# Routing of the last chunks inside the last pair's passes, the block table ahead of the last bound, x1 loaded during the blocks, 16 result tiles in the gather stage

## The chip, the cores and the metric

The kernel runs on one core of a Trainium2 chip. The metric is the device time of one execution in microseconds (us). Work is spread over the engines of the core: TensorE (PE in the profile; PEld is its loading of weights), VectorE (DVE), ScalarE (ACT), GpSimd (POOL) and SyncE (SP), which here only issues DMAs. DMAs are issued from SP's queue (SPq), ACT's (ACTq) and POOL's. Each engine takes its instructions in order; semaphores tie the engines together.

## The reference, cut to what matters

One transformer block on `x` of 4 sequences x 1024 tokens x 256 channels, modulated by a condition vector:

```
h = layernorm(x) * (1 + ca) + sa
x = x + ga * attn(h)            # gated delta rule, 16 heads of 64
h = layernorm(x) * (1 + cb) + sb
x = x + gb * ffn(h)             # mixture of 8 experts, the best 2 per token

# attn: q, k, v = silu(causal conv of 4 taps (h W)); k normalised; per step
S = clip(a_t * S + b_t * (v_t - a_t * S k_t) k_t^T, -5, 5);   o_t = S q_t
out = (o * silu(h Wg + bg)) Wo

# ffn: the two largest of 8 router logits, softmax over these two
y_e = gelu(h w1_e + b1_e) w2_e + b2_e;    out = p_1 y_e1 + p_2 y_e2
```

The kernel leaves the clip out and proves along the way that it never acts: a bound on every entry of S is carried through the sequence, and the flag `ok` says at the end whether the bound stayed under the limit. Only if it did not, a slow second program (`steps`, `experts`) runs after everything else.

## The kernel before, in words

**Chunks and pairs.** The tokens are cut into 32 chunks; a chunk is 32 tokens of each of the 4 sequences, that is 128 rows on the 128 partitions. Two chunks make a pair, and there are 16 pairs. The loop over the pairs in `chunks` runs several streams side by side: the preparation of the next pair (projections, decays, triangles), the passes through the state of this pair (`z`, `u`, `o`, S, `yT`, `ps_w`, and at the end of a chunk the sum `x<-x,add` at L1036), and the bounds (`ps_ut`, `sides`, the scans at L1096, `worst` at L1104). A stream is a Python generator; a string `PLAN` of one letter per step says which stream issues its next step. So the order of the instructions on PE, DVE, ACT and POOL within this part is written out by hand, and an instruction that waits holds whatever stands behind it on its engine. For the last pair there is nothing to prepare, and only passes, bounds and the streams `l` and `x` remain in the plan. After it come the last chunk's outputs, its `finish` and its bounds.

**Routing.** A finished chunk gets its second layernorm (`statistics`, `normed`, `modulated`), its router logits (`ps_h2`, `ps_l`), the two best experts, its places in the experts' lists (`ps_rk`, a count of the rows before it; `next` carries the counts on from chunk to chunk) and two indirect DMAs that write its 128 rows into `rows_scratch`, one for each expert (L394). The pair loop does this for the chunks finished in the pair before, within the preparation of the next pair. As the last pair prepares nothing, five chunks, 27 to 31, are left over, and they are routed after the last bounds, two at a time, since `ln2_h` has two buffers.

**The flag.** `ext`, `nul` and `ok` (L1202 to L1207) add up `worst` and look for values of S that are not finite; `ps_ok` and `n_safe` turn the flag into a number that the engines load at the very end.

**Blocks.** `blocks` makes a table (L1567 to L1633): how many blocks of 256 rows each expert has, and for each of 39 blocks its expert and its first row. SP loads the two numbers of each block from the table and with them issues the loads of the rows (`hb`, L1649), the weights (`w`, L1651 and L1653) and biases (`b`, L1655 and L1657), three buffers of each. PE transposes the rows (`ps_t`, L1663), multiplies by `w1` (`ps_hm`, L1670), ACT applies Gelu (L1677), PE multiplies by `w2` (`ps_yb`, L1682), DVE adds the bias (L1686), and POOL's queue writes the result to `outs_scratch` (L1687). Rows, logits' differences and the gate lie on other partitions than the last stage wants them, so small DMAs on ACT's queue copy them, eight for each of `at_out`, `dif_out` and `gate_out` (L1641).

**Gathers.** For each of the 32 chunks, two indirect DMAs on POOL fetch the two results of its 128 tokens (`y`, L1699), ACT and DVE weight and add them (L1705 to L1710) to `x1o`, which SP loads from `x_out_scratch` (L1695), and ACT's queue stores the sum (L1711). Each of these tiles has four buffers. The weights `prob` come from a sigmoid on ACT (L1692), whose function table is another than Gelu's.

The instructions of `blocks` are put in order by a scheduler, those of `chunks` not. A DMA that SP or ACT issues signals on one of eight semaphores, which the program goes round; an issue waits until the DMA before it on the same semaphore has landed. POOL's indirect DMAs have eight such semaphores of their own.

## Time and profile before

| | us |
|---|---|
| runs before the change, median (lowest to highest) | 2398.57 (2388.15 to 2409.16) |
| the profiled execution's own time | 2395.64 |
| its span | 2393.9 |
| last sum of chunk 31 (L1036) ends | 1906.5 |
| last bounds end (L1104) | 1926.6 |
| chunks 27 to 31 routed on DVE | 1924.9 to 1972.9 |
| first load of the first block | 1984.30 |
| last write of a block's result is issued | 2291.08 |
| first and last gather | 2296.02, 2382.79 |

All times within the profile are counted from the start of the span. The page of the profile gives busy time by engine and the costliest groups of instructions; the timeline gives the single rows, each with its start, its duration, and in brackets the idle time of its engine just before it and what ended that. Over the whole span PE is busy for 76% and DVE for 67%, but the shares differ by stage: until about 1900 several engines share the work, from 1995 to 2291 PE is nearly always busy, and after 2291 it stands still. The clock that TensorE was granted is 0.834 of full speed in the mean.

### The profile page before, as it was taken

The numbers are of one execution on the slowest core, as the hardware profiler recorded it, in microseconds if no ns is written. First come the engines' busy times: TensorE is split into PE (matmuls) and PEld (weight loads), VectorE is DVE, ScalarE is ACT, GpSimd is POOL, SyncE is SP. The second block draws the span as 40 slices with busy tenths as digits, with TensorE's granted clock in tenths as the row PEclk, the third lists the DMA queues.
The fourth block names the chain that finished last, engine by engine and source line by source line (L and its number), as shares of the span: only waits on it lengthen the run. The fifth ranks groups of instructions, "written<-read, shape, count | busy, mean of one in ns | idle before, by whom it ended". The sixth has DMA issues, their size and how long they took to land.

```text
span 2393.9 us, 96754 instructions
## 1 busy us (share of the span) xinstructions
PE 1816.4 (76%) x42550; PEld 1471.7 (61%) x42550; DVE 1598.0 (67%) x3170; ACT 1008.6 (42%) x2005; POOL 1079.2 (45%) x1189
## 2 busy tenths in 40 slices
PE   5777878787878787878787878878786627999920
PEld 3566666566657675666666666766675516888820
DVE  4768687878887878788787878887876332111133
ACT  3343545464545545454545453645453212222211
POOL 1115354647464645456454546464736630000055
PEclk7778889898989898989787888989797758999965
DMA  5523342435353434345343424232323106666645
GB/s 153 155 53 92 92 123 78 140 88 148 92 140 95 134 91 133 98 140 134 92 131 93 120 70 105 85 101 71 97 76 80 42 19 228 226 223 225 216 124 163
DMA packets 321248, 285.37 MB, mean 119 GB/s; under 512 B 112243, under 2 KB 279283, under 8 KB 320435
## 3 DMA queue, kind: packets, MB, share of 16 engines
q1 hardware_dynamic: 304946, 245.08, 36.0%
q0 software_dynamic: 9264, 27.01, 3.3%
q8 instruction: 337, 5.52, 0.9%
q10 hardware_dynamic: 6608, 7.00, 0.9%
q14 instruction: 93, 0.75, 0.1%
HBM read 215.09 MB, written 67.90 MB: 118 GB/s over the span
## 4 chain that ended last, share of the span: by engine, by line
PE 54%; issue 13%; DVE 9%; POOL 8%; ACT 7%; DMA 6%; SPq 2%; another core or an unknown queue 0%; ACTq 0%; POOLq 0%; DVEq 0%
PE ps_q L431 16%; PE ps_hm L1670 6%; PE ps_yb L1682 5%; PE ps_w L1025 3%; PE ps_gt L579 3%; PE ps_kk L647 3%; DMA sc<-g_scratch 3%; PE ps_t L810 3%; PE ps_u L923 2%; PE ps_s L955 2%; DVE kq L443 2%; POOL kq L792 2%; POOL aS L993 2%; PE ps_o L974 2%; PE ps_t L822 1%
## 5 line engine op out<-in xcount | busy, mean ns | idle before, releaser
L443 DVE SCALAR_TENSOR_TENSOR kq<-ps_q,w_conv,kq 128x256 f32<-128x256 f32 x768 | 362.6, 482 | 133.2 <-ACT kq L441 113.2
L431 PE MATMUL ps_q<-hT,w_kq 128*128 128x280 f32 x1024 | 364.7, 506 | 31.5 <-issue 12.0
L431 PEld LDWEIGHTS ps_q<-hT,w_kq 128*128 128x128 f32 x1024 | 232.7, 241 | 109.1 <-issue 21.2
L443 DVE SCALAR_TENSOR_TENSOR v<-ps_q,w_conv,v 128x256 f32<-128x256 f32 x384 | 185.1, 482 | 69.6 <-ACT v L441 59.2
L441 ACT ACTIVATE kq<-ps_q,w_conv 128x256 f32<-128x256 f32 x256 | 143.5, 563 | 200.4 <-PE ps_q L431 198.6
L792 POOL TENSOR_TENSOR kq<-kq,sc 128x512 f32<-128x512 f32 x128 | 177.1, 1404 | 87.4 <-DMA sc<-g_scratch 63.8
L1096 DVE TENSOR_TENSOR_SCAN sides<-aR,sides 128x512 f32<-128x512 f32 x128 | 189.8, 1482 | 37.0 <-POOL sides L1089 36.1
L1088 POOL TENSOR_TENSOR sides<-sides,least 128x512 f32<-128x512 f32 x128 | 193.7, 1513 | 10.0
L431 PE MATMUL ps_q<-hT,w_v 128*128 128x280 f32 x512 | 166.3, 451 | 41.1 <-ACT least L1073 22.6
L1686 DVE TENSOR_TENSOR yb<-ps_yb,b 128x256 f32<-128x256 f32 x78 | 33.1, 425 | 243.8 <-PE ps_yb L1682 243.8
L993 POOL TENSOR_TENSOR aS<-S,last 128x1024 f32<-128x1024 f32 x64 | 128.5, 2008 | 132.5 <-DVE S L962 128.4
L1085 POOL TENSOR_TENSOR sides<-sides,kR 128x512 f32<-128x512 f32 x128 | 166.4, 1300 | 17.4 <-ACT sides L1071 17.3
L1677 ACT ACTIVATE hm<-ps_hm,b 128x256 f32<-128x256 f32 x156 | 73.8, 473 | 221.0 <-PE ps_hm L1670 217.1
L1687 POOL DMA_DIRECT2D outs_scratch<-yb x39 | 27.9, 716 | 285.8 <-DVE yb L1686 276.1
L1670 PE MATMUL ps_hm<-hT,w 128*128 128x256 f32 x624 | 145.1, 386 | 8.5 <-DVE hT L1665 8.5
L579 PE MATMUL ps_gt<-hT,w_gt 128*128 128x256 f32 x512 | 147.4, 411 | 4.4 <-issue 3.1
L1682 PE MATMUL ps_yb<-w,hm 128*128 128x256 f32 x624 | 141.0, 379 | 0.0
L431 PEld LDWEIGHTS ps_q<-hT,w_v 128*128 128x128 f32 x512 | 96.8, 207 | 70.7 <-ACT least L1073 34.5
L810 PE MATMUL ps_t<-Tn,kd 32*32 32x16 f32 x4096 | 63.9, 210 | 96.2 <-issue 56.1
L1670 PEld LDWEIGHTS ps_hm<-hT,w 128*128 128x128 f32 x624 | 118.2, 192 | 29.2 <-DVE hT L1665 13.6
L394 POOL DMA_INDIRECT rows_scratch<-ln_h,at x64 | 64.9, 1015 | 153.3 <-DVE at L391 77.4
L441 ACT ACTIVATE v<-ps_q,w_conv 128x256 f32<-128x256 f32 x128 | 71.9, 562 | 146.6 <-PE ps_q L431 139.2
(211 smaller groups left out, 3953.1 us busy)
## 6 DMA issues: line engine op xcount, KB each, us to landing
w<-in_w SPq DMA_DIRECT2D x78, 512.0 KB
rows_scratch<-zero_row SPq DMA_DIRECT2D x34, 1024.0 KB
w_kq<-in_w_qkv SPq DMA_DIRECT2D x260, 128.0 KB
sc<-g_scratch SPq DMA_DIRECT2D x128, 256.0 KB
w_v<-in_w_qkv SPq DMA_DIRECT2D x129, 128.0 KB
w_gt<-in_w_g SPq DMA_DIRECT2D x258, 64.0 KB
aR<-g_scratch SPq DMA_DIRECT2D x128, 128.0 KB
kR<-g_scratch SPq DMA_DIRECT2D x128, 128.0 KB
```

The source lines that it names most:

```text
L431: nc.tensor.matmul(ps.rearrange("p y t -> p (y t)"), lhsT=w[:, dc], rhs=h_t[:, dc].rearrange("p x b t -> p (x b t)"), start=(dc == 0), sto ...
L441: nc.scalar.activation(o, tap(0), AF.Identity, scale=taps[:, 0:1], bias=taps[:, KC : KC + 1])
L443: nc.vector.scalar_tensor_tensor(o, tap(j), taps[:, j : j + 1], o, op0=ALU.mult, op1=ALU.add)
L579: nc.tensor.matmul(ps, lhsT=wg[:, dc], rhs=self.h_t[:, dc, :, :, KC - 1 :].rearrange("p x b t -> p (x b) t"), start=(dc == 0), stop=(dc == 1),
L792: nc.gpsimd.tensor_tensor(o, o, sc[:, h4 : h4 + 4], ALU.mult)
L810: nc.tensor.matmul(ps[q, n], lhsT=kd[q, n], rhs=Tn[q, n], start=True, stop=True)
L993: nc.gpsimd.tensor_tensor(aS.rearrange("q b h i -> q (b h) i"), S[:, bs].rearrange("q b h i -> q (b h) i"), self.pair.last[self.par][:, bs ...
L1085: nc.gpsimd.tensor_tensor(grow, grow, kR.rearrange("q h b t -> q h (b t)"), ALU.mult)
L1088: nc.gpsimd.tensor_tensor(grow, grow, least, (ALU.subtract, ALU.add)[y])
L1096: nc.vector.tensor_tensor_scan(f, aR.rearrange("q h b t -> q (h b t)"), f, 0.0, ALU.mult, ALU.add)
L1670: nc.tensor.matmul(ps, lhsT=w1[:, dc, fc * P : (fc + 1) * P], rhs=hT[:, dc], start=(dc == 0), stop=(dc == 1),)
L1682: nc.tensor.matmul(ps, lhsT=hm[:, fc, s * P : (s + 1) * P], rhs=w2[:, fc], start=(fc == 0), stop=(fc == 3),)
```

## The change

Four things are changed.

1. *Routing.* A new generator `sent` routes finished chunks one step at a time. In the last pair every second step of the plan is followed by one step of `sent`: first the two chunks that were finished before this pair (27 and 28, together), then 29 and 30, as they get finished. What is left of it runs after the last `finish`, and then the whole routing of chunk 31.
2. *The table* is made by `Routes.plan` in a tile that the chunks no longer need, after the routing of chunk 31 and ahead of the last bounds. The rows' numbers are corrected in place. `ps_ok` and `n_safe` are computed after the blocks and gathers.
3. *x1* is loaded on ACT's queue in eight DMAs of 512 KB, four chunks each, into tiles of their own; `prob` follows them. Both stand ahead of the blocks in the program. SP's order is now as the program has it.
4. *Gathers.* `y` has 16 buffers of two rows' worth each; the sums are made in the x1 tiles, and SP stores them.

Besides, `c0` of the bounds has one buffer instead of two.

```diff
     chunks(tc, a, nch, con, ones, modt, modc, x1_dram, rt)
     blocks(tc, a, nch, con, modt, rt, out)
+    with tc.tile_pool(name="n_ps", bufs=1, space=PSUM) as pp:
+        ps = pp.tile([1, 1], F32, name="ps_ok")
+        nc.tensor.matmul(ps, lhsT=rt.ok[:, 0:1], rhs=ones[:, 0:1], start=True, stop=True)
+        nc.vector.tensor_copy(n_safe, ps)
...
+    def plan(self, room):
...
+        table = pool.tile([1, NB, 2], I32, name="table")
+        nc.vector.tensor_copy(table[:, :, 0], of[0:1])
+        nc.vector.tensor_copy(table[:, :, 1], row[0:1])
...
+        nc.vector.tensor_tensor(mine_row, mine_row, atf, ALU.subtract)
+        self.table = table
...
-                c0 = take(s2, [P, 2, 4, B], "c0")
+                c0 = take(s1, [P, 2, 4, B], "c0")
...
+    def sent(chunks, last):
+        while True:
+            if chunks:
+                stat = statistics([x for _, x in chunks])
+                yield
+                hs = [normed(x, stat(i), "ln2_h") for i, (_, x) in enumerate(chunks)]
+                close("rs", "nm")
+                yield
+                for h in hs:
+                    modulated(h)
+                yield
+                yield from routing(chunks, hs)
+                if chunks[-1][0] == last:
+                    return
+            while not finished:
+                yield
+            chunks = [finished.pop(0)]
...
+        after, finished[:] = list(finished), []
         if g + 1 < npair:
-            after, finished[:] = list(finished), []
...
-        work(streams, PLAN)
-    for part in (prev.outputs, prev.finish, prev.bounds):
-        for _ in part():
+            work(streams, PLAN)
+        else:
+            sending = sent(after, nch - 2)
+            for i, name in enumerate(name for name in PLAN if name in streams):
+                next(streams[name], None)
+                if i % 2:
+                    next(sending, None)
+            work(streams, "")
+    for part in (prev.outputs(), prev.finish(), sending, sent([], nch - 1)):
+        for _ in part:
             pass
-    after = list(finished)
-    stat = statistics([x for _, x in after])
-    for i in range(0, len(after), 2):
-        two = after[i : i + 2]
-        hs = [modulated(normed(x, stat(i + j), "ln2_h")) for j, (_, x) in enumerate(two)]
-        for _ in routing(two, hs):
-            pass
-    ok = s1.tile([P, 2], F32, name="ok")
+    rt.plan(take(s2, [P, NH * 2 * TC * B], "plan", tag="kq", bufs=2))
+    close("kq")
+    for _ in prev.bounds():
+        pass
+    ok = rt.ok
...
-    cp = ctx.enter_context(tc.tile_pool(name="b_co", bufs=4))
+    cp = ctx.enter_context(tc.tile_pool(name="b_co", bufs=16))
...
+    NG = 4
+    x1 = []
+    for c in range(0, nch, NG):
+        x1.append(kp.tile([P, NG, D], F32, name=f"x1_{c}"))
+        nc.scalar.dma_start(x1[-1], rt.x1[c : c + NG].rearrange("c p d -> p c d"))
+    prob = kp.tile([P, 2, nch], F32, name="prob")
+    for k, sign in enumerate((1.0, -1.0)):
+        nc.scalar.activation(prob[:, k], dif, AF.Sigmoid, scale=sign)
+    E = mybir.EngineType
+    ctx.enter_context(tc.manual_schedule(engines={E.SP}))
...
     for c in range(nch):
-        x1 = cp.tile([P, D], F32, name="x1o")
-        nc.sync.dma_start(x1, rt.x1[c])
-        y = []
+        g, i = divmod(c, NG)
+        y = cp.tile([P, 2, D], F32, name="y")
         for k in range(2):
-            y.append(cp.tile([P, D], F32, name=f"y{k}"))
             nc.gpsimd.indirect_dma_start(
-                out=y[k],
+                out=y[:, k],
...
-        nc.vector.tensor_tensor(x1, x1, y[0], ALU.add)
-        nc.scalar.dma_start(out[c], x1)
+        nc.vector.tensor_tensor(x1[g][:, i], x1[g][:, i], y[:, 0], ALU.add)
+        nc.sync.dma_start(out[c], x1[g][:, i])
```

## The prediction

> **What bounds the kernel now.** I read the window table first, cut at the stages, because the shares of the whole span mix stages with different limits. Columns: stretch, its length, then busy us and count of PE, PEld, DVE, ACT, POOL, granted clock, DMA share, GB/s.
>
> ```profile
> 1838.00:1906.00 68.00, 50.08 (x1623) 42.12 (x1622) 25.26 (x19) 21.12 (x41) 36.36 (x40) 0.74 0.13 42
> 1906.00:1927.00 21.00, 0.13 (x2) 0.00 (x0) 8.80 (x11) 5.91 (x12) 14.69 (x19) 0.62 0.04 12
> 1927.00:1982.00 55.00, 13.47 (x52) 10.69 (x52) 19.21 (x99) 8.07 (x23) 18.58 (x21) 0.50 0.10 34
> 1995.00:2291.00 296.00, 287.60 (x1383) 249.71 (x1382) 57.58 (x116) 72.24 (x153) 27.22 (x38) 1.00 0.66 216
> 2291.00:2394.00 103.00, 0.00 (x0) 0.00 (x0) 39.45 (x96) 16.13 (x32) 63.41 (x65) 0.51 0.55 161
> ```
>
> The reader is to see that the blocks (1995 to 2291) fill PE, that in the gather stage nothing but POOL is near busy, and that between 1906 and 1982 no engine is: 76 us of a serial chain. So three places count: that chain, the first block, the gathers. The timeline gives their edges (start, duration, engine, line, operation, idle before it and its releaser):
>
> ```profile
> 1905.80 0.72 POOL L1036 TENSOR_TENSOR x<-x,add 128x256 f32<-128x256 f32 x1 [8.75 <-DVE add L1034]
> 1929.94 1.09 ACT L329 ACTIVATE ln_h<-x,nm,rs 128x256 f32<-128x256 f32 x2 [3.37 <-DVE nm L322]
> 1938.19 1.07 POOL L394 DMA_INDIRECT rows_scratch<-ln_h,at  x1 [4.56 <-DVE at L391]
> 1940.93 0.96 POOL L394 DMA_INDIRECT rows_scratch<-ln_h,at  x1 [1.67 <-DMA rows_scratch<-ln_h,at]
> 1972.05 3.72 ACTq L1641 DMA_DIRECT2D dif_out<-dif_all  x6
> 1984.30 0.42 SPq L1649 DMA_DIRECT2D hb<-rows_scratch  x1
> 1989.19 5.56 PE L1670 MATMUL ps_hm<-hT,w 128*128 128x256 f32 x16 [0.80 <-DVE hT L1665]
> 1991.33 1.28 ACT L1677 ACT_TABLE_LOAD   x1 [9.99 <-DMA hb<-rows_scratch]
> 1994.59 3.62 PE L1682 MATMUL ps_yb<-w,hm 128*128 128x256 f32 x16
> 2296.02 1.04 POOL L1699 DMA_INDIRECT y<-outs_scratch,at_out  x1 [4.23 <-issue]
> 2366.14 1.00 POOL L1699 DMA_INDIRECT y<-outs_scratch,at_out  x1 [1.80 <-DVE x1o L1710]
> 2382.79 0.95 POOL L1699 DMA_INDIRECT y<-outs_scratch,at_out  x1 [0.30 <-remote]
> ```
>
> Chunk 31 is finished at 1906.5; the last bounds fill POOL from there to 1926.6 (20.1 us); then five chunks are routed until 1972.9; the first block's load is issued at 1984.30. Before the last gathers POOL is held up; the list of what POOL waits for says how much (total, times, longest):
>
> ```profile
> POOL y L1699 <- issue: 18.7, 43, 4.2
> POOL y L1699 <- DVE x1o L1710: 5.1, 9, 1.8
> POOL y L1699 <- DVE y L1706: 3.3, 6, 1.8
> ```
>
> **Step 1: from the last finish to the first block's load.** Now this takes 1984.3 − 1906.5 = 77.8 us. In the changed program the four chunks 27 to 30 are meant to go before the last finish; behind it stay, in POOL's and DVE's order: chunk 31's routing, the table, the bounds, `ok`, the load. Chunk 31 alone: statistics and `rs`, `nm` about 2.5 us (from the rows at 1924.88 to 1929.94, less four chunks' statistics); from 1929.94 to the first row write at 1938.19, 8.25 us; the second write ends at 1941.89, 3.7 us later. Together 14.4. The bounds follow on POOL: 20.1. The table (7.7 us of DVE rows between 1968.99 and 1981.3) runs beside them, and SP has read its entries early; but the first `hb` load still waits for the bounds' last ACT operation and for `ok`, because its memory is that of the chunks' tiles. After that ACT operation come `ext` 0.21, `nul` 1.22, its sum 2.28, `ok` 0.4: 4.2. With under 1 us to the load the path is 14.4 + 20.1 + 4.2 + 0.8 = 39.5 instead of 77.8: **38.3 us less, if the last finish doesn't move**. The table ahead of the bounds is worth only what of it is on the path, some 4 us of that; `ok` is late next.
>
> **Step 2: it does move.** Four routings go into the last pair's 68 us, and the engines take orders as written, so a step of a routing that waits holds what is behind it. Each adds about 6 us to POOL (1.2 + 2 x 0.72 + 2 x 1.0 + the 1.67 between the two writes), 3 to DVE, 1.3 to ACT, 2.8 to PE. POOL is idle 31 of the 68 us, so the sum alone would fit. The walk through the new order, with the durations of the trace, does not:
> - chunk 27: `ps_rk` and `hT2` before `ps_w`: first S update +1.8 us; the two row writes stand before the next `aS` on POOL: +3.
> - chunk 28: `ps_l` waits on PE for ACT's copy in front of `ps_ut` and the second `ps_s`: second S update and the `z` copies +4.
> - chunk 29: PE meets `ps_h2` before `ps_u`, while its POOL steps stand behind half of the bounds (`sides`, 2.8 us) and behind chunk 28's writes: `ps_u` +10; then `ps_rk` waits behind DVE's `add` of chunk 30: +12.
> - chunk 30: `ps_h2` and `ps_l` stand before `ps_y`, again with POOL's steps behind half of the bounds: +14.
>
> So the last finish moves by **14 us** to about 1920. Also chunk 30's second half (`top` to the row writes) stands behind chunk 31's `add` on DVE and its writes before chunk 31's `rs` on POOL: 4.8 us more behind the finish. From 38.3 remain 38.3 − 14 − 4.8 = **19.5 us**; the load would be issued at 1965. Bounds: if every wait falls into idle time the finish moves by 4 us and 30 is left; if each of the four costs its whole 9.6 us (1972.9 − 1924.9 over five), nothing is left. The value taken is the walk's.
>
> **Step 3: the first block.** ACT now issues, behind `ok` and ahead of everything of the blocks: 24 small copies (`at`, `dif`, `gate`), eight `x1` loads of 512 KB, a table load, two `prob`, and only then the table load and the first Gelu. An issue on ACT's queue takes 3.72 / 6 = 0.62 us (row at 1972.05); 32 of them 19.8. Table loads and `prob`: 1.28 + 0.6 + 1.28 = 3.2. The DMAs of SP and ACT go round eight semaphores, each waiting for the one before on its own; the seventh `x1` load so waits for the third to land, which with the weights beside it (2.6 MB at the 280 to 370 GB/s around 2000 us) is up to 4 us more. First Gelu 22.5 to 27 us after the `hb` load, against 1992.62 − 1984.30 = 8.3 now. PE has `ps_hm` of block 0 and the transposes of blocks 1 to 3 to do meanwhile, then waits. `ps_yb` of block 0 starts some 1 us behind the first Gelu, 23.5 to 28 after the load against 10.3 now: 13 to 18 late; the three transposes done early give back 1.6; `ps_yb` on a PE that stood still costs about 5.56 − 3.62 = 1.9 more, as `ps_hm` does now. **+15.5 us.** If ACT's issues overlapped with the wait for `ok`, this would fall to 5; they can't, the first waits for it too. The `x1` loads end before block 3 needs its weights, so the blocks after that keep their 15.30 us for two (`ps_yb` at 2011.28 and at 2026.58): 0, at most 5 us for 4.2 MB at those rates. SP's order by hand leaves the blocks' own order of loads.
>
> The Trainium skill, "DMA: Bandwidth & Descriptors", section "Issuing engines are not separate DMA queues", holds against this step: the engines that issue share the same DMA engines, and issuing from several saves only issue time, usually small beside the DMA. By that ACT's 32 issues would weigh little and the sum would end near 2370 us; the row at 1972.05 has 0.62 us for a copy of a few KB, and that is what I go by. The skill's "TensorE: Matmul & The Clock Gate", section "HAM oscillation — how this bites in real kernels", says that a PE idle for longer than about 3.4 us starts again at the slow clock; the trace agrees in kind (granted clock 0.50 from 1984 to 1989, 1.00 from 1995 on). An estimate from that page's two clocks, 1.2 and 2.4 GHz, is 3.6 us more for `ps_yb`, and 2387 instead of 2385.
>
> **Step 4: gathers.** 64 gathers, issue to issue 0.95 + 0.30 = 1.25 us where nothing holds them; 45 in a row took 2296.02 to 2352.29, 1.28 each. The later ones lost 5.8 us in idle times above 0.30, which the list puts down mostly to DVE: four buffers, and `x1o` loads that come late. With 16 buffers and `x1` at hand: 63 x 1.28 = 80.6 instead of 86.8, **−6.2**. The tail from the last gather to the end (11.1 us) keeps its steps; the out stores go from ACT's queue to SP's, which is idle. Bounds: 0 (POOL's own pace, and the DMA share, unchanged) to −9 (1.25 each, and a shorter tail). `ps_ok` and `n_safe` behind the blocks: one matmul and one cast of under 0.2 us beside idle engines, 0. `c0` with one buffer: written and read by POOL alone, in order, 0.
>
> **Sum**, on the profiled execution's 2395.64 us: −19.5 + 15.5 − 6.2 = −10.2, so 2385.4. That execution lies 2.9 us under the median of the runs shown; half of that added, I say **2387 us**. About 1% (24 us) is what a measurement of this kernel can tell from no change.
>
> **Rivals.**
> - *The routing hides well.* Finish 4 us late, chunk 30 not behind: −34 with 13 for the first block and −6: 2369. For it: POOL's 31 idle us, DVE's 43. Against: PE and POOL meet those waits in a fixed order.
> - *Nothing is hidden* (the other side). The four routings in the last pair cost their full 9.6 us each, by the in-order waits of PE and POOL; step 1 gives 0, the first block's 15.5 stay, gathers −6.2: 2405, slower. It decides from where the finish and chunk 30 together take more than about 29 us of the 38.3. For it: each routing is a chain of a dozen hand-overs, and the walk counts few of their latencies. Against: half the last pair is idle on three engines.
> - *The gathers don't gain* (the DMA share is 0.65 between 2300 and 2350, though no wait there ends on a DMA but one), all else as forecast: 2393.
> - *The change doesn't do what it says*: the table ahead of the last bound doesn't start the blocks, since `hb` waits for `ok`; this is in the forecast, not beside it.
>
> **Chances.** Forecast 0.46, hidden well 0.22, nothing hidden 0.2, no gain in the gathers 0.12. The range goes from the hidden-well case, 2369, to nothing hidden, 2404. Faster by over 1% is most of the second case, 0.2; slower by over 1% needs nothing hidden and 15 us more of a stall: 0.08; the rest 0.72.
>
> **What would show it.** The last `x` sum of chunk 31 at about 1920 (1910: hidden well; over 1935: nothing hidden); ACT's `worst` at 1960; the first `hb` load at 1965; the first Gelu 22 to 27 us behind it, with ACT's queue full of issues between; 15.3 us for two blocks; 64 gathers at 1.25 to 1.3 with no wait on DVE. It is wrong if ACT's issues don't hold the Gelu, or if the walk through the last pair missed waits.

## The result and the profile after

The changed kernel takes 2398.42 us (median; 2385.07 to 2412.89), the kernel before, run beside it, 2395.06 (2378.32 to 2414.7). The ratio is 1.002, 95% interval 1.0007 to 1.0033: a little slower, where 10 us less had been forecast. The profiled execution takes 2392.86 us (span 2391.1). That is 2.8 us less than the one before, but only because its part up to the last pair, which the change doesn't touch, happened to be 8 us shorter: the last pair's first `aS` starts at 1808.46 here and at 1816.49 before. All stages are therefore counted from that row.

The window table of the changed kernel, cut at its stages: the last pair from 21.5 us behind its first `aS`, the chain up to the first block's load, the first block up to `ps_yb`, the blocks, the gathers. Columns as in the table before.

```profile
1830.00:1913.00 83.00, 57.92 (x1616) 48.24 (x1608) 31.59 (x69) 23.38 (x51) 45.37 (x52) 0.72 0.14 44
1913.00:1959.00 46.00, 5.11 (x22) 4.16 (x22) 22.86 (x60) 7.60 (x17) 21.37 (x25) 0.54 0.05 18
1959.00:1992.00 33.00, 9.79 (x32) 7.07 (x32) 2.08 (x3) 3.34 (x6) 0.00 (x0) 0.60 0.76 249
1992.00:2288.00 296.00, 288.08 (x1374) 250.24 (x1374) 56.45 (x115) 73.22 (x156) 28.26 (x39) 0.99 0.65 212
2288.00:2391.00 103.00, 0.00 (x0) 0.00 (x0) 38.07 (x96) 16.24 (x32) 63.30 (x65) 0.51 0.42 126
```

The reader is to see that the last pair's row has grown from 68 to 83 us, that the serial chain of 76 us (two rows before) has shrunk to 46, and that 33 us lie between the first load and the blocks, where it was 13 (1982 to 1995 before); in them DMA is at 0.76 and no engine is busy for a third. The blocks keep their 296 us and the gathers their 103. The timeline has the edges (most rows of PE, DVE and SP between them are left out):

```profile
1912.22 0.72 POOL L1129 TENSOR_TENSOR x<-x,add 128x256 f32<-128x256 f32 x1 [8.34 <-DVE top L453]
...
1958.76 0.62 ACTq L1681 DMA_DIRECT2D dif_out<-dif_all  x1
1958.89 0.44 SPq L1700 DMA_DIRECT2D hb<-rows_scratch  x1
1959.47 5.78 ACTq L1681 DMA_DIRECT2D at_out<-at_b  x8
1965.36 4.38 ACTq L1681 DMA_DIRECT2D dif_out<-dif_all  x7
1969.79 6.07 ACTq L1681 DMA_DIRECT2D gate_out<-modt  x8
1975.89 12.70 ACTq L1687 DMA_DIRECT2D x<-x_out_scratch  x8
1988.62 1.28 ACT L1690 ACT_TABLE_LOAD   x1 [33.84 <-DMA x<-x_out_scratch]
...
1991.58 1.57 ACT L1728 ACTIVATE hm<-ps_hm,b 128x256 f32<-128x256 f32 x4
...
1992.10 5.41 PE L1733 MATMUL ps_yb<-w,hm 128*128 128x256 f32 x16 [1.12 <-ACT hm L1728]
...
2293.44 1.06 POOL L1745 DMA_INDIRECT y<-outs_scratch,at_out  x1 [5.22 <-issue]
```

The first block's load comes 17 us sooner than before, counted from `aS` (14 in the second pair of profiles below), but the first Gelu comes 33 us behind it, since 32 issues on ACT's queue stand ahead of it. Both kernels were profiled once more (see `r_before`, `r_after`); the steps of the prediction against the two pairs of profiles, each time the difference after less before in us:

| step | forecast | first pair | second pair |
|---|---|---|---|
| 2: end of chunk 31's last `x` sum, from the last pair's first `aS` | +14 | +14.5 | +17.3 |
| 1: from there to the first `hb` load (77.8 before) | −33.5 | −31.8 | −31.6 |
| 3: from there to the first `ps_yb` (10.3 before) | +15.5 | +22.9 | +23.5 |
| blocks: to the issue of the last result's write | 0 | −1.1 | +0.3 |
| to the first gather | 0 | +1.0 | +0.2 |
| 4: first gather to the end | −6.2 | −0.2 | −0.5 |
| sum | −10.2 | +5.2 | +9.1 |

The sums, +0.22% and +0.38%, agree with the timed +0.20% and, beside the second pair, +0.34%.

### The profile page after: what moved, and what is told of

Read it like the earlier page. It is cut to its first block, busy times and chain, and to the rows that moved or that the text cites. A ratio compares the mean times of both kernels' runs of the same rounds, so it can differ in the third digit from the quotient of the medians.

```text
span 2391.1 us, 96650 instructions
## 1 busy us (share of the span) xinstructions
PE 1809.2 (76%) x42550; PEld 1465.4 (61%) x42550; DVE 1601.5 (67%) x3176; ACT 1009.8 (42%) x2005; POOL 1084.0 (45%) x1192
## 5 line engine op out<-in xcount | busy, mean ns | idle before, releaser
L524 PE MATMUL ps_q<-hT,w_kq 128*128 128x280 f32 x1024 | 357.0, 497 | 32.6 <-issue 11.5
L524 PEld LDWEIGHTS ps_q<-hT,w_kq 128*128 128x128 f32 x1024 | 227.5, 236 | 108.6 <-issue 23.0
L1189 DVE TENSOR_TENSOR_SCAN sides<-aR,sides 128x512 f32<-128x512 f32 x128 | 187.2, 1464 | 22.6 <-POOL sides L1182 21.7
```

What stands on the lines that cost most here:

```text
L524: nc.tensor.matmul(ps.rearrange("p y t -> p (y t)"), lhsT=w[:, dc], rhs=h_t[:, dc].rearrange("p x b t -> p (x b t)"), start=(dc == 0), sto ...
L1189: nc.vector.tensor_tensor_scan(f, aR.rearrange("q h b t -> q (h b t)"), f, 0.0, ALU.mult, ALU.add)
```

## The experiments

"Finish" is the end of chunk 31's last `x` sum, counted from the last pair's first `aS`. Unless a text says otherwise the edit is made in the changed kernel. Ratios are to the kernel before, with their 95% intervals.

### The first block: what holds ACT

```diff
-        nc.scalar.dma_start(x1[-1], rt.x1[c : c + NG]...)
+        later.append((x1[-1], rt.x1[c : c + NG]...))
...                                   # in block i, behind the load of b2
+        if i >= 4 and later:
+            nc.sync.dma_start(*later.pop(0))
```

> The changed kernel with the eight x1 loads taken from ACT's queue and issued by SP, one behind the loads of each of the blocks 4 to 11; nothing else. Theory A (ACT's queue holds the first Gelu: 32.7 us behind the first hb load, of which the eight x1 issues take 12.7): first Gelu about 20 us behind the hb load, first ps_yb 12 us earlier, the blocks behind it at 15.3 us for two as before; in all 10 to 13 us less than the changed kernel, a ratio to the kernel before of about 0.997. Theory B (it is the 4.2 MB of x1 beside the weights that delay block 0 to 3, whoever issues them): the first ps_yb comes earlier, but blocks 4 to 11 lose what it gains; ratio 1.002 as now.

```diff
-            nc.scalar.dma_start(there, here)
+            copies.append((there, here))
...
+    later += copies                   # prob: behind the blocks in the program
```

> As the kernel with x1 on SP, and the 24 small copies (at, dif, gate) issued by SP too, one per block from block 12 on, and the sigmoid for prob placed behind the blocks in the program (the scheduler puts it among the last third of them, with two table loads of 1.28 us). ACT has nothing ahead of the first Gelu but its table load. Theory A: first Gelu 8 to 9 us behind the first hb load, as before the change, first ps_yb 21 to 23 us earlier than in the changed kernel, up to 3 us lost once at the sigmoid; in all 18 to 22 us less than the changed kernel, ratio to the kernel before about 0.993. Theory B: not below 0.998.

Measured: 0.993 (0.9905 to 0.9956) and 0.991 (0.9878 to 0.9942). ACT's timeline with only the x1 loads moved:

```profile
1972.13 0.61 ACTq L1681 DMA_DIRECT2D dif_out<-dif_all  x1
...
1983.53 5.94 ACTq L1681 DMA_DIRECT2D gate_out<-modt  x8
1989.50 1.28 ACT L1690 ACT_TABLE_LOAD   x1 [21.35 <-DMA gate_out<-modt]
...
1992.45 1.57 ACT L1730 ACTIVATE hm<-ps_hm,b 128x256 f32<-128x256 f32 x4
```

and with the copies moved as well:

```profile
1969.91 1.15 ACT L1197 ACTIVATE sides<-sides,unsafe 128x1024 f32<-128x1024 f32 x1
...
1982.18 1.28 ACT L1729 ACT_TABLE_LOAD   x1 [11.02 <-PE ps_hm L1722]
1983.47 0.85 ACT L1729 ACTIVATE hm<-ps_hm,b 128x256 f32<-128x256 f32 x2
```

What releases the table load changes from the last DMA to `ps_hm`. The first Gelu comes 32.7 us behind the first `hb` load in the changed kernel, 20.2 without the x1 issues, 8.2 without any, as in the kernel before (8.3); the first `ps_yb` 33.2, 20.7 and 10.6. So what stood on ACT ahead of the Gelu is the whole of the delay: 12.5 us of it go with the eight x1 loads, 10.1 with the 24 copies and with `prob`, whose table load and two sigmoids (1.7 us) were moved along with them. The blocks take 296.6 us in the second run with all 32 DMAs spread over them: beside the blocks these transfers cost nothing that can be seen. The first of the two ratios is better than the 0.997 expected, and its interval ends below that: the timed gain is larger than the 12.5 us of the first block. The changed kernel itself was not timed on the chip of these two runs, so where the rest comes from stays open.

Why eight x1 issues take 12.7 us is in the changed kernel's first profile. First their own durations (ns: least, median, most), then the rows of the second to the seventh:

```profile
L1687 ACTq DMA_DIRECT2D x<-x_out_scratch x8: 365/442/977, 1975.9 to 1987.6; - x8
```

```profile
1976.53 1.08 ACTq L1687 DMA_DIRECT2D x<-x_out_scratch  x2
1978.47 0.36 ACTq L1687 DMA_DIRECT2D x<-x_out_scratch  x1
1981.28 0.37 ACTq L1687 DMA_DIRECT2D x<-x_out_scratch  x1
1983.41 0.37 ACTq L1687 DMA_DIRECT2D x<-x_out_scratch  x1
1987.20 0.37 ACTq L1687 DMA_DIRECT2D x<-x_out_scratch  x1
```

The issues themselves are short, 4.1 us for all eight. The other 8.6 us are nearly all waits ahead of the fourth to the seventh: 0.86, 2.45, 1.76 and 3.42 us. In the profile's record of semaphores each of these four starts 0.02 to 0.03 us after the DMA before it on its own semaphore has landed (1978.44, 1981.26, 1983.39, 1987.18). For the seventh that is the third x1 load; for the fourth, fifth and sixth it is a load of SP's, the rows and the two weights of the third block, since SP and ACT go round the same eight semaphores. Over all 32 issues from 1958.76 to 1988.59 the issues take 18.1 us and the waits between them 11.8; in the second profile 20.9 (two x1 issues take 2.24 and 1.43 us there) and 9.4.

### The gathers

The whole gain of step 4 rested on POOL's waits before. Each kernel was profiled again:

> The kernel before, unchanged, profiled once more. Its gather stage ended 97.9 us behind the first gather, with DVE's starts on the 0.70 us grid from the 57th us of the stage on. In the kernels profiled on the chip of the later runs that stretch is missing (end at 91 to 94). If the stretch belongs to a program: it is there again, DVE's last sum at 92 to 93 behind the first gather. If it comes and goes with the chip or the execution: it may be missing; then the stage of this kernel without it shows what four buffers and the x1 loads cost (about 87 to 89 to the last sum, by POOL's 86.8).

> The changed kernel, unchanged, profiled once more beside the others of this call. Same question: if the slow stretch belongs to the program, DVE's last sum comes 92 to 93 us behind the first gather; if not, at 86 as in the kernel with four buffers. The rest as before: last finish 104 to 108 us behind the aS of the pair's start, first hb load 46 behind that, first ps_yb 33 behind the load; ratio 1.002, or 0.2% less where the stretch is missing in it and not in the kernel before.

The kernel before, one execution: 2406.9 us. The changed one: 1.0034 (1.0007 to 1.006). What POOL waits for in the gathers (total, times, longest), in the first profile of the changed kernel and then in the second profile of the kernel before:

```profile
POOL y L1745 <- DVE x L1756: 0.9, 3, 0.3
```

```profile
POOL y L1699 <- DVE x1o L1710: 3.3, 11, 0.3
POOL y L1699 <- DVE y L1709: 2.4, 8, 0.3
```

In the second profile of the kernel before the name "DVE x1o" is still there, but the longest wait is 0.3 us, POOL's own gap between two gathers: nothing is late. In it the last gather starts 81.00 us after the first and the end comes at 91.88 (86.77 and 97.88 in the first profile); in the changed kernel 81.60 and 91.35. So the 5.8 us of stalls that the forecast meant to take away are not there in every execution of the kernel before. What it was is seen on DVE. This is DVE's timeline in the first profile of the changed kernel, which has it too:

```profile
2362.56 0.43 DVE L1756 TENSOR_TENSOR x<-x,y 128x256 f32<-128x256 f32 x1 [1.97 <-remote]
2363.26 0.42 DVE L1755 TENSOR_TENSOR y<-y,gate_out 128x256 f32<-128x256 f32 x1 [0.28 <-DVE x L1756]
...
2366.77 0.42 DVE L1756 TENSOR_TENSOR x<-x,y 128x256 f32<-128x256 f32 x1 [2.69 <-remote]
2368.16 0.42 DVE L1755 TENSOR_TENSOR y<-y,gate_out 128x256 f32<-128x256 f32 x1 [0.96 <-issue]
```

and the second profile of the changed kernel, at the same place of the program:

```profile
2377.61 0.48 DVE L1752 SCALAR_TENSOR_TENSOR y<-y,prob 128x256 f32<-128x256 f32 x1 [1.19 <-DMA y<-outs_scratch,at_out]
2378.01 0.42 DVE L1756 TENSOR_TENSOR x<-x,y 128x256 f32<-128x256 f32 x1
2378.35 0.42 DVE L1755 TENSOR_TENSOR y<-y,gate_out 128x256 f32<-128x256 f32 x1
```

In the first, operations of 0.42 us that depend only on DVE's own earlier work start at steps of 0.70 us or multiples of it (0.70, 3.51, 1.39 between the rows shown), for some 25 us. In the second, the operations come in threes, the weighting and the gate of one chunk and between them the sum of the chunk before, one behind the other as soon as a gather has landed. The stretch shows in 5 of 18 profiles and in both kernels: in both first ones, whose chip is not on record, and in three of the four experiments on the chip numbered 9; in none of the twelve profiles on the chips 6 and 3, the two second ones among them. So it doesn't belong to either program, but whether it comes with the chip or with the execution is not shown. With four buffers it holds POOL up, as in the first profile of before; with 16 POOL runs through (last gather at 81.3) but the sums come late all the same, and the end is at 97.7 instead of 97.9.

Whether the buffers are worth anything without the stretch:

```diff
-    cp = ctx.enter_context(tc.tile_pool(name="b_co", bufs=16))
+    cp = ctx.enter_context(tc.tile_pool(name="b_co", bufs=4))
```

> The changed kernel with 4 instead of 16 buffers of gathered results, x1 still loaded ahead. If DVE paces the gather stage: POOL's last gather moves back towards 86 us behind the first, the last DVE sum stays at 92 to 93 behind the first gather and the span ends 97 to 99 behind it, as with 16. If the buffers are what matters: last sum 4 us or more later.

2414.41 us in a single execution, where the kernel before had a median of 2400.53; no stretch in its profile, last gather at 82.06, end at 91.59, against 81.60 and 91.35 with 16. Nothing is gained by the 16. Two more runs tried DVE's side, one with fewer, larger operations, one with as many more small ones:

```diff
+        some, x = y4[:, lo : lo + n, 0], x1[g][:, lo : lo + n]     # n = 4 chunks
+        nc.vector.tensor_tensor(some, some, gate...to_broadcast([P, n, D]), ALU.mult)
+        nc.vector.tensor_tensor(x, x, some, ALU.add)
```

> The changed kernel with the gather stage's products with the gate and its sums with x1 made for four chunks in one DVE instruction each (the last four chunks one by one), 42 DVE instructions fewer, the same elements; four buffers of four chunks instead of sixteen of one. Theory C (the gather stage is paced by DVE, whose instructions from about 60 us into the stage on start on a grid of 0.70 us without a wait for another engine): fewer instructions end earlier: last DVE sum at 86 to 88 us behind the first gather instead of 92.4, end of the span 4 to 6 us earlier, ratio about 1.000. Theory D (DVE's time goes by elements, or by what POOL writes at the same time): last sum at 92 as now or later, ratio 1.002 or more.

```diff
+        nc.vector.memset(idle[:, 0:1], 0.0)       # per chunk, a tile that nobody reads
+        nc.vector.memset(idle[:, 1:2], 0.0)
```

> The changed kernel with 64 tiny DVE instructions more (memsets of one column of a tile that nothing reads); the scheduler puts them among the blocks, where DVE is idle. In the runs so far DVE's starts fall on the 0.70 us grid from about its instruction 3466 on, for some 30 instructions, whatever the kernel; with 63 more instructions ahead of the first gather that stretch would begin at chunk 6 or 7 of the gather stage instead of chunk 22. Theory C1 (a stretch of the instruction stream at a fixed place starts slowly): DVE is 8 us late by chunk 14, catches up behind it, last DVE sum at 86 to 88 us behind the first gather instead of 92.4, end of the span about 5 us earlier than in the changed kernel although it does more. Theory C2 (slow from that instruction on to the end): last sum beyond 105 us. Theory D (what POOL writes beside it, or the time): last sum at 92 to 93 as now, the slow stretch at the end.

Neither has the stretch. Sums of four: 0.9998 (0.9972 to 1.0025), the last gather at 85.1, since POOL's gathers themselves became slower: the mean of one is 1045 ns, and 980 to 997 in the other 17 profiles. Its last sum comes at 89.7, where the three others on chip 9, with the stretch, have 92.5 to 93.0; whether the larger operations kept the stretch away or it was missing by chance, one profile can't tell. The run with more small operations (2411.25 us in a single execution) was to move the stretch to an earlier place by putting 64 operations among the blocks. On its chip no kernel has the stretch, so it decides nothing; its gathers, 86.2 to the last sum, are those of the unchanged program. Another try was both weightings on ACT, on top of the version with all issues moved:

```diff
-        nc.scalar.mul(y[:, 0], y[:, 0], prob[:, 0, c : c + 1])
-        nc.vector.scalar_tensor_tensor(y[:, 0], y[:, 1], prob[...], y[:, 0], ...)
+        for k in range(2):
+            nc.scalar.mul(y[:, k], y[:, k], prob[:, k, c : c + 1])
+        nc.vector.tensor_tensor(y[:, 0], y[:, 0], y[:, 1], ALU.add)
```

> The kernel with x1 and the copies on SP, and in the gather stage both weightings on ACT, so that DVE only adds the two, multiplies by the gate and adds x1: one semaphore instruction less per chunk on DVE, 3474 instructions in all instead of 3506, of which only the last few lie in the slow stretch. Theory C1: last DVE sum 86 to 88 us behind the first gather, 5 us less than the kernel it is made from; ratio to the kernel before about 0.990. Theory D: as that kernel, 92 to 93, or later for ACT's second operation (0.5 us a chunk, beside idle time).

0.9932 (0.9903 to 0.9961); last sum at 86.85 and end at 94.01, 2.7 us later than in the second profile of the changed kernel: a longer tail and no gain. The four kernels further below that also have it end at 92.7 to 93.1; the seven profiles without it, without the stretch and with single sums at 91.4 to 92.1.

### The last pair: what delays its finish

First, all of `sent` behind the pair instead of between its passes:

```diff
-                if i % 2:
-                    next(sending, None)
```

> The changed kernel without the steps of the routing between the last pair's passes: chunks 27 to 30 are routed by the same generator behind the last finish, ahead of chunk 31. Theory W (the walk: the steps hold PE and POOL, 14.4 us on the last finish, and still hide most of four routings): the last finish comes back by 14 us, to 90 us behind the aS of the pair's start that stood at 1808.46; behind it come 18 us for two chunks and 14 for each of two, less the 5 that chunk 30 cost already, so the first hb load is 22 to 27 us later than in the changed kernel, ratio 1.011. Theory N (nothing is hidden by the steps): hb load and time as in the changed kernel, ratio 1.002.

1.0089 (1.0057 to 1.0122). The finish falls to 87.1 us, but the first `hb` load comes 85.1 us behind it instead of 46: together 21.8 and 18.6 us more than in the two profiles of the changed kernel. The interleaving is worth its delay. Where the delay sits was foreseen on PE (chunk 29's `ps_h2` is `ps_h` L439 in the profile). PE's waits for the modulated rows, second profile of the changed kernel (chunks 29 and 30):

```profile
1890.13 0.69 PE L439 MATMUL ps_h<-consts,ln_h 128*128 128x128 f32 x2 [9.76 <-POOL ln_h L428]
...
1917.64 0.69 PE L439 MATMUL ps_h<-consts,ln_h 128*128 128x128 f32 x2 [5.31 <-POOL ln_h L428]
```

If PE's place were the cause, one step later would do:

```diff
                 for h in hs:
                     modulated(h)
                 yield
+                yield
```

> The changed kernel with one more empty step in the routing between the modulated rows and their transposition, so that everything behind it comes one step (two of the plan) later: ps_h2 of chunk 29 stands behind ps_u and ps_w instead of ahead of ps_u, ps_h2 of chunk 30 behind ps_w, and the row writes of chunk 29 behind the second aS. The same instructions, other places. Theory W (it is the places where PE and POOL meet a routing step that isn't ready that cost the 14 to 18 us): last finish at 93 to 97 us behind the aS instead of 104 to 108; 3 to 6 us of chunk 30 more behind the finish; first hb load 6 to 10 us earlier in all, ratio to the kernel before about 0.998. Theory S (the sum of the work put into the last pair costs, wherever it stands): finish at 104 to 108 as now, ratio 1.002 or more.

1.0023 (0.9995 to 1.0051), finish at 107.5: unchanged. PE in that kernel:

```profile
1882.96 0.69 PE L439 MATMUL ps_h<-consts,ln_h 128*128 128x128 f32 x2 [6.97 <-POOL ln_h L428]
1908.56 6.50 PE L1118 MATMUL ps_w<-w_o,yT 128*128 128x256 f32 x16 [11.66 <-DVE yT L1107]
```

Chunk 30's wait for `ln_h` is gone, and an idle time of 11.66 us for DVE's `yT` stands ahead of `ps_w` in its place. That theory fell. The other: POOL is too late with `modulated`, which stands in its order behind row writes and halves of the bounds. So the two operations were given to DVE, for the chunks that `sent` routes:

```diff
-    def modulated(h):
-        nc.gpsimd.tensor_tensor(h, h, modt[:, CB], ALU.mult)
-        nc.gpsimd.tensor_tensor(h, h, modt[:, SB], ALU.add)
+    def modulated(h, eng=nc.gpsimd):
+        eng.tensor_tensor(h, h, modt[:, CB], ALU.mult)
+        eng.tensor_tensor(h, h, modt[:, SB], ALU.add)
...
-                    modulated(h)
+                    modulated(h, nc.vector)
```

> The changed kernel, but in `sent` the two operations of `modulated` (times and plus the condition's rows) run on DVE instead of POOL. Theory Q (the last pair's delay belongs to POOL's order: `modulated` of chunks 29 and 30 stands behind half of the bounds): PE's waits for `ln_h`, 9.8 and 5.3 us in the second profile of the changed kernel, shrink to about 5 and 2, since only `rs` still stands behind POOL's row writes; the last x sum ends 97 to 103 us after the pair's first aS instead of 105 to 108, and the whole is 4 to 9 us shorter. Theory H (the hand-overs between DVE, ACT and PE hold it, whatever engine modulates): DVE now waits for ACT's `ln_h` in its own order and holds the scans behind; the sum stays at 105 to 109, the time within 2 us of the changed kernel's.

```profile
1884.34 0.66 PE L439 MATMUL ps_h<-consts,ln_h 128*128 128x128 f32 x2 [4.64 <-DVE ln_h L428]
...
1909.47 0.69 PE L439 MATMUL ps_h<-consts,ln_h 128*128 128x128 f32 x2 [3.01 <-DVE ln_h L428]
```

0.9974 (0.9946 to 1.0002). PE's two waits shrink from 9.76 and 5.31 to 4.64 and 3.01 us, 7.4 together, and the finish comes at 99.0 instead of 107.5, sooner than in any of the nine profiles in which the last pair is that of the changed kernel (101.2 to 107.8; their spread, 4 us of it there already at chunk 29's sum, is one of executions). Counted from chunk 29's sum, the finish comes at 58.2 us, against 64.6 in the second profile of the changed kernel and 62.0 to 66.1 in the nine. So 6.4 of the 8.5 us arise behind chunk 29's sum, and 3.8 lie beyond the lowest of the nine. The rows ahead of chunk 29's `ps_h` say what POOL's part was, in the second profile of the changed kernel and then with `modulated` on DVE:

```profile
1883.73 0.60 ACT L422 ACTIVATE ln_h<-x,nm,rs 128x256 f32<-128x256 f32 x1
...
1887.75 0.72 POOL L427 TENSOR_TENSOR ln_h<-ln_h,modt 128x256 f32<-128x256 f32 x1
```

```profile
1882.67 0.60 ACT L422 ACTIVATE ln_h<-x,nm,rs 128x256 f32<-128x256 f32 x1 [0.48 <-DVE nm L415]
1883.30 0.42 DVE L427 TENSOR_TENSOR ln_h<-ln_h,modt 128x256 f32<-128x256 f32 x1 [0.67 <-ACT ln_h L422]
```

On POOL, `ln_h` lies ready for 3.4 us (1884.33 to 1887.75) while POOL, by its order, waits for `sides` and works on it, and the two operations then take 2.3 us (0.72 and 1.52, a gap between); on DVE they start at once and take 0.9. For chunk 30 it is 2.5 us of lying and 2.3 of work on POOL, 1.1 and 1.8 on DVE. So the way to `ps_h` gets shorter by 4.7 and 2.0 us, 4.8 of them together by POOL's order and the rest by its speed. That is as the theory of POOL's order has it, with a smaller share for its speed. The 4.64 and 3.01 that remain, and some 9 us of finish over the kernel before, are the rest of the hand-overs, which no run took apart.

### The table ahead of the last bounds

```diff
-    rt.plan(...)
-    close("kq")
     for _ in prev.bounds():
         pass
+    rt.plan(...)
+    close("kq")
```

> The changed kernel with the table of blocks made behind the last bounds instead of ahead of them, ahead of ok, all else the same. The theory of the prediction (the blocks' first load waits for ok, so the early table is worth only what would stand on the path behind the bounds, now hidden): from the last finish to the first hb load 46 us become 50 to 55. Rival (the table is what starts the blocks): 7.7 us of table and the reading of its numbers by SP come on top whole, 56 us or more. A third: the scans of the bounds were held by the table, which takes its place: 46.

2399.95 us in a single execution; the load comes 50.9 us behind the finish, not 46.1: the table's place is worth 4.8 us of the path, about the 4 of the prediction. The timeline of the second profile of the changed kernel shows what is late next:

```profile
1971.49 0.22 DVE L1318 TENSOR_REDUCE ext<-worst 128x1 f32<-128x64 f32 x1 [1.65 <-ACT sides L1197]
1971.62 1.22 DVE L1320 TENSOR_SCALAR nul<-S 128x2048 f32<-128x2048 f32 x1
1972.88 2.29 DVE L1321 TENSOR_REDUCE ext<-nul 128x1 f32<-128x2048 f32 x1
...
1975.57 0.44 SPq L1700 DMA_DIRECT2D hb<-rows_scratch  x1
```

The last bound, the flag, the load. What SP waited for ahead of that load (total, times, longest):

```profile
SPq L1700 <- DVE ok L1322: 22.6, 1, 22.6
```

So the memory of the blocks comes free with `ok`, and the next version moved the bounds and the flag.

### A version that beats both

All issues on SP during the blocks, both weightings on ACT, and the end of the chunks in another order:

```diff
-    for part in (prev.outputs(), prev.finish(), sending, sent([], nch - 1)):
-        ...
-    rt.plan(...)
-    ... bounds, ext, nul, ok
+    go(bounds, 2); outputs; nul and its sum; go(finish, 1); go(bounds, 2)
+    go(finish, 2); rest of sending; go(bounds, 3); go(last, 1); go(bounds, 2)
+    go(last, 2); go(bounds, 2); rest of last; rest of bounds
+    rt.plan(...); ext of worst; ok         # last = sent([], nch - 1)
```

`go(part, n)` issues the next n steps of a part. In the first of these runs `sent` has the additional step of above.

> All that paid, and the end of the chunks in another order: the empty step in the routing; x1 and copies on SP; both weightings of the gather stage on ACT; half of the last bounds ahead of the last finish, where POOL is idle during ps_w, the other half between the steps of chunk 31's routing; the check of S for ok ahead of the last finish; the table behind the scans. By the theories: finish 94 to 98 us behind the aS; first hb load 28 to 32 behind the finish instead of 46 (chunk 30's rest 10, chunk 31 9, scans 2.4, table 7.7, ok 0.6); first ps_yb 10.5 behind the load; gather stage's end 92 to 94 behind the first gather. In all some 45 us less than the changed kernel, ratio to the kernel before about 0.982. If the bounds ahead of the finish hold POOL's last x sum, the finish comes up to 5 us later, 0.984.

> All parts together, as in the run with everything, but without the additional step between modulation and routing: x1 loads and small copies on SP during the blocks, both weightings on ACT, the end of the chunks reordered so that the last bounds fill POOL's waits. Both theories: the finish stays at 105 to 109, the first hb load comes 26 to 30 us behind it, first Gelu 8.5 us behind that; about 36 us less than the changed kernel, 2365 to 2372. If the additional step helped within the combination, 3 us and more slower than that run's 0.985.

> All parts together with the additional step, and modulation of the routed chunks on DVE. Theory Q: last x sum at 98 to 104 instead of 107.9, chunk 31's own routing 1 us shorter too; 2357 to 2363, ratio 0.981 to 0.984. Theory H: 107 to 110, ratio 0.985 to 0.987.

> All parts together without the additional step, modulation of the routed chunks on DVE. Theory Q: the last x sum as in the changed kernel with modulation on DVE, 97 to 103, and the ratio 0.980 to 0.984. Theory H: 105 to 109, ratio 0.985 to 0.987.

| run | ratio, 95% | median us | finish | finish to `hb` load |
|---|---|---|---|---|
| `e11_all_together` | 0.9851 (0.9815 to 0.9887) | 2366.81 | 107.9 | 28.0 |
| `e13_all_but_later` | 0.9865 (0.9812 to 0.9919) | 2362.18 | 103.4 | 27.6 |
| `e14_all_and_dve` | 0.9826 (0.9759 to 0.9893) | 2357.00 | 101.5 | 27.6 |
| `e15_all_dve_no_later` | 0.9834 (0.9781 to 0.9888) | 2354.98 | 103.7 | 27.6 |

The window table of the last of them, cut at the same stages:

```profile
1833.00:1916.00 83.00, 60.57 (x1679) 50.58 (x1680) 39.93 (x76) 26.15 (x57) 50.63 (x57) 0.70 0.14 44
1916.00:1943.00 27.00, 2.99 (x13) 2.19 (x11) 17.58 (x55) 5.86 (x14) 12.03 (x14) 0.52 0.09 29
1943.00:1953.00 10.00, 5.87 (x19) 4.76 (x20) 1.05 (x4) 2.54 (x4) 0.00 (x0) 0.59 0.83 247
1953.00:2250.00 297.00, 288.37 (x1388) 250.65 (x1387) 57.74 (x117) 75.18 (x158) 27.41 (x39) 1.00 0.70 231
2250.00:2348.00 98.00, 0.00 (x0) 0.00 (x0) 35.58 (x96) 32.48 (x64) 63.80 (x65) 0.51 0.43 132
```

The chain behind the finish is down to 27 us from 46, the first block's stretch to 10 from 33. All four are 1.3% to 1.7% under the kernel before; among themselves they can't be told apart by time. The first had been expected to finish at 94 to 98 and the last at 97 to 103; neither did. The modulation on DVE moves the finish by 6.4 us with the additional step and not at all without it. These are single profiles, and nine profiles of one last pair lay 6.6 us apart, so neither difference is shown. One possible reason: in this order of the end, halves of the bounds stand ahead of the last chunk's outputs, and may hold the finish too; that was not tested by itself.

## Why the prediction was wrong

**Step 1, the load: the mechanism right, the sum 1.7 us too good.** Finish to load was forecast at 44.3 and is 45.95 and 46.1; `ok` is late next, as said; the table's place is worth 4.8 us against "some 4 us".

**Step 2, the finish: right in its sum, half right in its reason.** +14 forecast, +14.5 and +17.3 measured; the nine profiles of that last pair spread from +11 to +18, so that the sum comes so close in the first is partly luck. Chunk 29's `ps_h2` waits on PE ahead of `ps_u` as walked, 8.26 us in the first profile and 9.76 in the second for the walk's "`ps_u` +10". The walk gave two reasons, the place on PE and POOL's steps behind half of the bounds. The place isn't what sets it, since moving it only moved the wait; POOL's order is, with its speed, for some 6 to 8.5 of the 17.3 us, by single profiles.

**Step 3, the first block: the step that failed by its size.** "+15.5 us" measured 22.9 and 23.5. The term that was too small is the wait for semaphores. For the issues themselves the forecast had 0.62 us each, "32 of them 19.8", and that was about right: 18.1 and 20.9 us in the two profiles. For the semaphores it had "up to 4 us more", by one wait, that of the seventh x1 load for the third. That wait is there, 3.4 us in both profiles, and three others are not in the sum: the fourth, fifth and sixth x1 load wait 5.1 us (2.6 in the second profile) for SP's loads of the third block, which use the same semaphores; the copies, taken without a wait, wait another 3.1 and 3.3. So from 1958.76 to 1988.59 it took 29.8 us instead of at most 23.8. Between 1976 and 1992 the DMA share is 0.98, and the x1 loads land 6.0 to 11.0 us after their issue. The forecast's "the first waits for it too" and its slow `ps_yb` (5.41 us against 3.62) were right.

The Trainium skill's "DMA: Bandwidth & Descriptors", section "Issuing engines are not separate DMA queues", calls issue time usually small relative to the DMA, and for one x1 load that agrees with the trace, 0.44 us (median) against 6.0 to 11.0 to its landing. What the prediction drew from it, that ACT's issues would then weigh little, doesn't hold: with `prob` and the issues gone from ACT the first Gelu comes 24.5 us sooner. The 3.6 us estimated from its "TensorE: Matmul & The Clock Gate", section "HAM oscillation — how this bites in real kernels", for `ps_yb` is too much: it lost 1.8. The granted clock was 0.50 up to 1995 and 1.00 from 1996 on, so only a part of `ps_yb`, which ran from 1992.10 to 1997.51, was slow, and the estimate took all of it.

**Step 4, the gathers: the step that failed in kind.** "With 16 buffers and `x1` at hand" the end was to come 6.2 us sooner; it came 0.2 and 0.5 us sooner. POOL's part came as forecast: its waits for DVE went (8.4 us put down to DVE, then 1.2), and its last gather starts 81.3 us behind the first where "80.6" had been said. What failed is "the tail from the last gather to the end (11.1 us) keeps its steps": it became 16.3 us, because DVE, in its slow stretch, was as late with the sums as before. POOL's waits before had needed that stretch. In the second pair there was nothing to remove: the kernel before has its last gather at 81.0 already. Where there is a stretch, DVE's sums end the kernel, with any number of buffers (92.4 to 93.0 us behind the first gather in all five profiles); where there is none, four buffers don't hold POOL (last gather at 81.0 and 82.1). The lower bound, 0 ("POOL's own pace, and the DMA share, unchanged"), was the right value. The rival *The gathers don't gain* had this outcome for another reason (the DMA share) and, with all else as forecast, 2393.

Steps 3 and 4 together miss the forecast by 13.4 and 13.7 us in the two pairs, of 15.4 and 19.3 in all; the rest is the last pair and its load. The measured time lies between the forecast and the rival *Nothing is hidden* (2405 by its own sum; the range ends at 2404), but not by that rival's way: with the routing behind the pair the load comes 18.6 to 21.8 us later, so that much was hidden. And 1% is not "what a measurement of this kernel can tell from no change": over 52 and 78 executions the interval of the ratio is 0.26% wide.

**Open** remain the cause of the stretch on DVE (its rows name "remote", "issue" or its own last operation; the profiles don't part chip from execution), and the second half of the finish's delay.

## What to carry to other kernels

A transfer that is needed late costs as much as one that is needed now if its issue stands ahead of the next stage's first operation on an in-order queue: 32 early issues on ACT, with `prob` behind them, took 22.6 us, more than the 14 to 17 that the moved routing had saved, while the same 32 on SP, one per block, cost nothing. To price such issues, count not only their own time but the DMA that holds each one's semaphore: here three of the four long waits were for another queue's loads. A stall that one profile shows late in a stage is a candidate, not a gain: profile the unchanged kernel a second time, if possible on another chip, and ask whether the operations that hold it have a cause in the program. And compare two profiles from a row common to both: the two executions here differed by 8 us before the change began.

## What was not expected of the hardware

- DVE ran stretches of some 25 us in which 0.42 us operations started only at multiples of 0.70 us, in 5 of 18 profiles: both first ones, three of four on chip 9, none of twelve on chips 6 and 3.
- An issue of a 512 KB load on ACT's queue took 0.37 to 0.98 us (up to 2.24 in the second profile), but waited up to 3.4 us for the DMA before it on its semaphore, three times out of four one that SP had issued. The DMA share was 0.98.
- Gathers on POOL took 1045 ns each beside DVE operations over four chunks' columns, in one profile, and 980 to 997 beside operations over one's.
